# A graph network's seam between two layers: the last layer norm ahead of the selections, other places for rows and casts, and a transpose left to a store

## The chip, the cores and the metric

The kernel runs on one core of a Trainium2 chip. The metric is the device time of one execution in microseconds (us), as a median over runs. One execution is also taken with the hardware profiler; all times inside the kernel come from that one and count from the start of its span.

The core has a matrix engine (TensorE, PE in the profile, with PEld for its weight loads), VectorE (DVE), ScalarE (ACT), GpSimd (POOL), SyncE (SP), and 16 DMA engines. Every engine works through its own list of instructions in order and waits on semaphores. In this kernel POOL and SP do little but issue transfers: SP the loads, POOL the stores.

## The reference

Two layers of a graph network act on 3327 nodes with 1024 features; `adj` is a 3327 x 3327 matrix, mostly zeros, with weights on its edges. Cut to what matters:

```python
# layer 0
h = maximum(layernorm(x), 0)
support = quantised(relu(quantised(h) @ quantised(weight)))
x = x + adj @ support * scales
# layer 1: graph attention, 8 heads of 64
h = maximum(layernorm(x), 0)
Wh = einsum('nf,hfd->hnd', h, W)
e_src, e_dst = (Wh . a1), (Wh . a2)              # one number per head and node
e = leaky_relu(e_src[:, :, None] + e_dst[:, None, :], 0.2)
att = softmax(where(adj > 0, e, -9e15), axis=-1)
enc = elu(einsum('hnm,hmd->hnd', att, Wh))       # heads side by side: 512 per node
x = x + mlp(enc)                                 # 512 -> 256 -> 256 -> 512 -> 1024
```

## The kernel before

The nodes are padded to 26 tiles of 128 rows. The work runs in four stages.

**Stage 1** (to about 147 us) makes the quantised support of all nodes, kept on chip as `s_int` (26 tiles). **Stage 2** (its last product ends at about 957 us; the heads of its last two tiles follow) loops over 26 tiles `t`. For each tile the product `adj @ support` (L443) runs over the 26 column tiles in four parts of 7, 6, 7 and 6. A part is loaded as `at` (SP, L177, three buffers), split into a rounded half `hi` (ACT, L179) and a rest `lo` (DVE, L183), and tested for edges into a byte mask `mk` (DVE, L184) that is stored to `mask_d` (POOL, L188). The product's result is scaled (L451, L452) and added to `xt` (L453), which is stored to `x1_d`. The function `normalised` (L145 to L152) then makes the layer norm `y`: statistics, six short steps on one column (`lnv`, a square root on ACT, `lnr`, `lnq`, ...), and one pass over the 1024 features.

`heads(t, y)` is called one tile late, so that tile `t - 1` goes through its heads while the product of tile `t` runs. It transposes `y` on PE (L380), copies with ReLU into `ht` (ACT, L381), multiplies with the weights of the heads (`whm`, 16 matmuls at L384), copies to `wht` (L386), and forms `src` and `dst` (DVE, L391 and L392): 8 numbers per node, one per head. `dst` goes negated into `ndst`, which stays on chip. `src` is transposed on PE (`sp`, L398), copied by ACT (`srct`, L400) and stored by POOL (L403), so that `src_d` holds one row per head. `src_d` is four arrays, for the four groups of tiles in `SUBS`. The features times exp(dst) are made (`ft`, L408 and L409), split into a rounded part and a rest (`fw`, L414 and L415) and stored to `feat_d` (L423); a reordered copy `dw` (L419) goes to `dsum_d` (L427).

**Stage 3** (its first selection starts at 968 us, its last product ends about 2003) is attention. It takes 32 passes, each for one head and one group of 7 or 6 destination tiles. In each pass a row of `src_d` is loaded to all partitions as `srow` (SP, L503). For each of the 26 source tiles `j`, DVE makes a selection `sel` (L617): the mask where `srow` exceeds `ndst[j]`, else zero. PE multiplies it into 7 or 6 accumulators `acc` (L626) with the features `f_even` or `f_odd` (L493). Between these, PE works through products over all edges, `mps` (L534), from `dw` and from masks that ACT casts to `mf` (L533); `edge_steps` writes out how many of them follow each `j`. `sel` has four buffers, `srow` two. After a pass the accumulators are copied to `xs` (L638) and finished by `close`. **Stage 4** is the MLP.

What engine does what is fixed in the program; the order in which each engine gets the instructions of neighbouring tiles and stages is set by a scheduler at build time from priorities and expected durations. So the selections of stage 3 can stand in DVE's list before the end of stage 2. `keep_in_program_order` and `issue_after` bind it. Stage 3's tiles lie in memory that stage 1 and 2 used: with `reuse_waits="tile"` a new tile waits for the last use of just those old tiles that it overlaps. Pools take their place in the order in which they are opened. In the kernel before the order is `f1`, `sel`, `srow`, `mf`, `md`, `s3`.

Of the kernel before, what the change touches and what calls it, by code (L numbers as in the profile page):

```python
# [1 line left out]

# [6 lines left out]
F32 = mybir.dt.float32  # L9
# [5 lines left out]
ALU = mybir.AluOpType  # L15
# [4 lines left out]
P = 128  # L20
# [7 lines left out]
NH = 8  # L28
# [14 lines left out]
SUBS = [range(0, 7), range(7, 13), range(13, 20), range(20, 26)]  # L43
# [16 lines left out]
def two_layer_kernel(  # L60
# [23 lines left out]
    nc = tc.nc  # L84
# [5 lines left out]
    ident = const.tile([P, P], F32, name="ident")  # L90
# [54 lines left out]
    def normalised(dst, src):  # L145

        stats = small.tile([P, FC, 6], F32, tag="stats", name="stats")
        statistics(stats, src)
        mv = small.tile([P, 2], F32, tag="mv", name="mv")
        nc.vector.bn_aggr(mv, stats.rearrange("p c s -> p (c s)"))  # L150
        r = inverse_std(mv[:, 1:2], 1, EPS, "ln")
        nc.vector.tensor_scalar(dst, src, mv[:, 0:1], r, ALU.subtract, ALU.mult)  # L152

    def normaliser(mv, n, eps, factor, tag):

# [12 lines left out]
    with tc.tile_pool(name="wh", bufs=1, reuse_waits="tile") as whp, tc.tile_pool(  # L168
# [201 lines left out]
        with tc.tile_pool(name="s2", bufs=2, reuse_waits="tile") as s2, tc.tile_pool(  # L370
            name="s2_tp", bufs=2, space=PSUM, reuse_waits="tile"
        ) as tp_ps, tc.tile_pool(name="s2_wh", bufs=2, space=PSUM, reuse_waits="tile") as wh_ps:

            def heads(t, h):
                ht = s2.tile([P, KF, P], F32, name="ht", bufs=1)
                for g in range(KF // 4):
                    tp = tp_ps.tile([P, 4, P], F32, tag="tp2", name="tp2")
                    for q in range(4):
                        k = 4 * g + q
                        nc.tensor.transpose(tp[:, q, :], h[:, k * P : (k + 1) * P], ident)  # L380
                    nc.scalar.activation(ht[:, 4 * g : 4 * g + 4, :], tp, AF.Relu)  # L381
                whm = wh_ps.tile([P, EMB], F32, name="whm")
                for k in range(KF):
                    nc.tensor.matmul(whm, ht[:, k, :], whead[:, k, :], start=(k == 0), stop=(k == KF - 1))  # L384
                wht = s2.tile([P, EMB], F32, name="wht", bufs=1)
                nc.scalar.copy(wht, whm)  # L386
                src = small.tile([P, NH], F32, name="src")
                dst = small.tile([P, NH], F32, name="dst")
                for a_t, e in ((a1_t, src), (a2_t, dst)):
                    prod = s2.tile([P, EMB], F32, name="prod", bufs=1)  # L390
                    nc.vector.tensor_tensor(prod, wht, a_t, ALU.mult)  # L391
                    nc.vector.tensor_reduce(  # L392
                        e, prod.rearrange("p (h d) -> p h d", d=HD), AX.X, ALU.add
                    )
                nc.vector.tensor_scalar(ndst[:, t], dst, -1.0, None, ALU.mult)
                nc.scalar.activation(ratio[:, t], src, AF.Exp, scale=1.0 - SLOPE)
                sp = tp_ps.tile([P, 4, P], F32, tag="tp2", name="sp")
                nc.tensor.transpose(sp[:NH, 0, :], src, ident)  # L398
                srct = s2.tile([NH, P], F32, name="srct")
                nc.scalar.copy(srct, sp[:NH, 0, :])  # L400
                for sub, d in zip(SUBS, src_d):
                    if t in sub:
                        nc.gpsimd.dma_start(d[:, (t - sub[0]) * P : (t - sub[0] + 1) * P], srct)  # L403

                ft = s2.tile([P, NH, 2, HC], F32, name="ft", bufs=1)
                wh3 = wht.rearrange("p (h d) -> p h d", d=HD)
                for q, slope in enumerate((1.0, SLOPE)):
                    nc.scalar.activation(ft[:, :, q, HD], dst, AF.Exp, scale=slope)  # L408
                    nc.vector.tensor_tensor(  # L409
                        ft[:, :, q, :HD], wh3, ft[:, :, q, HD:].to_broadcast([P, NH, HD]), ALU.mult  # L410
                    )
                fw = s2.tile([P, NH, 2, 2 * HC], F32R, name="fw", bufs=1)
                f2 = ft.rearrange("p h q c -> p h (q c)")
                nc.scalar.copy(fw[:, :, 0], f2)  # L414
                nc.vector.tensor_tensor(fw[:, :, 1], f2, fw[:, :, 0].bitcast(F32), ALU.subtract)  # L415

                dw = s2.tile([P, NPAIR, 2, 2, HC], F32R, name="dw", bufs=1)
                for q in range(2):
                    nc.scalar.copy(  # L419
                        dw[:, :, q],  # L420
                        fw[:, :, q, HC:].bitcast(F32).rearrange("p (g e) c -> p g e c", e=2),
                    )
                nc.gpsimd.dma_start(  # L423
                    feat_d[t].rearrange("h p c -> p h c"),
                    fw.bitcast(F32).rearrange("p h q c -> p h (q c)"),
                )
                nc.gpsimd.dma_start(  # L427
                    dsum_d[t].rearrange("g p c -> p g c"),
                    dw.bitcast(F32).rearrange("p g q e c -> p g (q e c)"),
                )  # L430

            before = None
            for t in range(T):
                xt = s2.tile([P, F], F32, name="xt2")
                load_rows(xt, x, t)
                mm = mm_ps.tile([P, F], F32, tag="mm", name="mm2")
                for js in PARTS:
                    hi, lo = part
                    part = next(columns, None)
                    for q, j in enumerate(js):  # L440
                        for which in (hi, lo):
                            for c in range(FC):
                                nc.tensor.matmul(  # L443
                                    mm[:, c * 512 : (c + 1) * 512],
                                    which[:, q, :],
                                    s_int[j][:, c * 512 : (c + 1) * 512],
                                    start=(j == 0 and which is hi),
                                    stop=(j == T - 1 and which is lo),
                                )
                y = s2.tile([P, F], F32, name="y")  # L450
                nc.scalar.activation(y, mm, AF.Copy, scale=r_asf)  # L451
                nc.vector.tensor_scalar(y, y, asf_t, sup_delta, ALU.mult, ALU.mult)  # L452
                nc.vector.tensor_tensor(xt, xt, y, ALU.add)  # L453
                nc.gpsimd.dma_start(x1_d[t * P : (t + 1) * P, :], xt)
                normalised(y, xt)
                if before is not None:
                    heads(*before)
                before = (t, y)
            heads(*before)
# [15 lines left out]
    LATE = 2 * T + START  # L475
    with ExitStack() as wide, tc.tile_pool(name="f1", bufs=1, reuse_waits="tile") as f1p, tc.tile_pool(
        name="sel", bufs=4, reuse_waits="tile"
    ) as selp, tc.tile_pool(name="srow", bufs=2, reuse_waits="tile") as srowp, tc.tile_pool(name="mf", bufs=2, reuse_waits="tile") as mfp, tc.tile_pool(
        name="md", bufs=2, reuse_waits="tile"
    ) as mdp, tc.tile_pool(name="s3", bufs=1, reuse_waits="tile") as s3, tc.tile_pool(  # L480
        name="s3_acc", bufs=7, space=PSUM, reuse_waits="tile"
    ) as acc_ps, tc.tile_pool(name="s3_m", bufs=1, space=PSUM, reuse_waits="tile") as m_ps:
        f_odd = f1p.tile([P, T, HW], F32R, name="f_odd")
# [11 lines left out]
        def load_mask(si, sub):  # L495
            for b, t in enumerate(sub):
                nc.sync.dma_start(masks[si][:, b], mask_d[t])

        def load_src(i):
            c, g, e, si = attends[i]  # L500
            nb = len(halves[c][si])
            srow = srowp.tile([P, 7, P], F32, name="srow")
            nc.sync.dma_start(  # L503
                srow[:, :nb].rearrange("p b i -> p (b i)"),
                src_d[2 * c + si][2 * g + e].partition_broadcast(P),
            )
            return srow
# [77 lines left out]
            )  # L585

        old, young = PARTS[:3], [range(20, 24), range(24, 25), range(25, 26)]
        load_mask(0, SUBS[0])
        srow = load_src(0)
        load_features(f_even, feat_d, 0, old)  # L590
        load_features(dw, dsum_d, 0, old)
        load_mask(1, SUBS[1])
# [4 lines left out]
        for i, (c, g, e, si) in enumerate(attends):  # L597
            h = 2 * g + e
# [5 lines left out]
            for j in range(T):  # L604
# [8 lines left out]
                if n in (STEPS * NPAIR - T, STEPS * NPAIR):  # L613
                    si1 = (n - (STEPS * NPAIR - T)) // T
                    load_mask(si1, halves[1][si1])
                sel = selp.tile([P, 7, P], F32R, tag="sel", name="sel")
                nc.vector.scalar_tensor_tensor(  # L617
                    sel[:, :nb],
                    srow[:, :nb],
                    ndst[:, j, h : h + 1],  # L620
                    mask[:, :, j, :],
                    ALU.is_gt,
                    ALU.mult,
                )
                for b in range(nb):
                    nc.tensor.matmul(  # L626
                        accs[b], sel[:, b, :], f[:, j, :], start=(j == 0), stop=(j == T - 1)
# [159 lines left out]
```

## Time and profile before

| What | us |
|---|---|
| median of 3 runs | 2317.66 (2315.4 to 2319.2) |
| the profiled execution, its own time | 2316.48 |
| its span in the profile | 2314.7 |
| PE busy | 2252.5 (97%) |
| DVE busy | 1567.1 (68%) |
| ACT busy | 1003.0 (43%) |
| POOL busy (issuing left out) | 119.0 (5%) |

The 1.8 us between the profiled time and the span lie outside the profile. A group's row in the profile gives the line of the kernel, the engine, the operation, output and inputs by the program's names, its busy time and its mean; after `<-` stands what released it from waiting. The name of an operand is that of its tile, with buffer numbers left out.

### The profile page before, as it was taken

To read this page: it belongs to the slowest core of one execution; us is meant where nothing else is said; L and a number is where in the kernel's file an instruction comes from. 1 tells how busy PE (TensorE), PEld (TensorE's weight loads), DVE (VectorE), ACT (ScalarE), POOL (GpSimd) and SP (SyncE) were. 2 spreads that over 40 slices of the span, in tenths; PEclk is the share of its full clock that TensorE was granted. 3 is DMA by queue.
4 is the path that set the end of the run, shared out by engine and by line. 5 is a ranking of instruction groups with operands and counts; after the bars stand their busy time and mean duration, and the time that the engine had idled before them with its cause. 6 is when DMAs were issued, how large, how long until landed. Compare 5 with 4: busy or idle time off the path is not lost. (4 is left out here: it accounts for less than half of the span.)

```text
span 2314.7 us, 32013 instructions
## 1 busy us (share of the span) xinstructions
PE 2252.5 (97%) x12884; PEld 1788.4 (77%) x12896; DVE 1567.1 (68%) x2090; ACT 1003.0 (43%) x1654; POOL 119.0 (5%) x173
## 2 busy tenths in 40 slices
PE   4999999999999999899999999999999999999999
PEld 2467777777777777589999999999999999644444
DVE  7845555555555555487999999999999999812211
ACT  4743334333333333346555555555555555311110
POOL 0000011011110110100000000000000000000000
PEclk9999999999999999999999999999999999999999
DMA  6324444444444444743324241545242332433311
GB/s 231 128 90 149 147 159 135 154 157 149 152 152 137 165 155 144 278 145 112 112 73 147 80 146 45 197 156 162 79 143 83 117 105 71 152 109 114 131 56 55
DMA packets 150302, 304.94 MB, mean 132 GB/s; under 512 B 10173, under 2 KB 91021, under 8 KB 150153
## 3 DMA queue, kind: packets, MB, share of 16 engines
q1 hardware_dynamic: 130248, 229.72, 29.7%
q0 software_dynamic: 19904, 73.17, 9.7%
q8 instruction: 101, 1.65, 0.3%
q14 instruction: 49, 0.39, 0.1%
HBM read 216.07 MB, written 86.79 MB: 131 GB/s over the span
## 5 line engine op out<-in xcount | busy, mean ns | idle before, releaser
L617 DVE SCALAR_TENSOR_TENSOR sel<-srow,ndst,mask 128x896 fp32r<-128x896 f32 (+1 forms) x832 | 869.6, 1082 | 61.2 <-PE acc L626 49.7
L534 PE MATMUL mps<-dw,mf 128*128 128x260 f32 x2704 | 462.7, 284 | 0.0
L443 PE MATMUL mm<-s_int,hi 128*128 128x512 f32 x1352 | 433.0, 399 | 0.0
L443 PE MATMUL mm<-s_int,lo 128*128 128x512 f32 x1352 | 421.6, 391 | 0.0
L626 PE MATMUL acc<-f_even,sel 128*128 128x260 f32 x2704 | 403.9, 284 | 1.4 <-DVE sel L617 1.3
L533 ACT CAST mf<-mask 128x1664 fp32r<-128x1664 uint8 x208 | 330.0, 1588 | 167.1 <-PE mps L534 129.3
L626 PE MATMUL acc<-f_odd,sel 128*128 128x260 f32 x2704 | 393.9, 285 | 6.9 <-DVE sel L617 6.8
L534 PEld LDWEIGHTS mps<-dw,mf 128*128 128x128 f32 x2704 | 379.8, 188 | 9.3 <-ACT part L538 8.4
L626 PEld LDWEIGHTS acc<-f_odd,sel 128*128 128x128 f32 x2704 | 352.6, 188 | 15.9 <-DVE sel L617 12.2
L626 PEld LDWEIGHTS acc<-f_even,sel 128*128 128x128 f32 x2704 | 356.7, 188 | 5.9 <-DVE sel L617 2.8
L443 PEld LDWEIGHTS mm<-s_int,lo 128*128 128x128 f32 x1352 | 253.8, 188 | 57.6 <-issue 5.7
L443 PEld LDWEIGHTS mm<-s_int,hi 128*128 128x128 f32 x1352 | 252.1, 188 | 55.6 <-issue 5.7
L184 DVE TENSOR_SCALAR mk<-at 128x896 uint8<-128x896 f32 x104 | 61.7, 593 | 262.6 <-DMA at<-in_adj_t 261.9
L179 ACT CAST hi<-at 128x896 fp32r<-128x896 f32 x104 | 92.7, 891 | 328.7 <-PE mm L443 294.8
L384 PE MATMUL whm<-whead,ht 128*128 128x512 f32 x416 | 186.9, 602 | 0.8 <-ACT ht L381 0.8
L731 PE MATMUL o<-weights,h 128*128 128x512 f32 x416 | 179.7, 592 | 0.0
L731 PEld LDWEIGHTS o<-weights,h 128*128 128x128 f32 x416 | 79.0, 190 | 99.1 <-issue 99.0
L384 PEld LDWEIGHTS whm<-whead,ht 128*128 128x128 f32 x416 | 77.5, 191 | 98.1 <-issue 87.7
L183 DVE TENSOR_TENSOR lo<-at,hi 128x896 fp32r<-128x896 f32 x104 | 106.6, 1025 | 51.3 <-ACT hi L179 39.9
L538 ACT COPY part<-mps 128x260 f32<-128x260 f32 x104 | 39.1, 376 | 216.3 <-PE mps L534 216.3
L741 DVE TENSOR_TENSOR yo<-o,nodes 128x1024 f32<-128x1024 f32 (+1 forms) x27 | 31.8, 1182 | 146.0 <-PE o L731 146.0
L332 PE MATMUL mm<-w_int,xqt 128*128 128x512 bf16 x404 | 98.3, 393 | 9.5 <-DVE w_int L319 7.3
(128 smaller groups left out, 1566.9 us busy)
## 6 DMA issues: line engine op xcount, KB each, us to landing
feat_d<-fw POOLq DMA_DIRECT2D x26, 1040.0 KB, 5.3
f_even<-feat_d SPq DMA_DIRECT2D x7, 3380.0 KB, 12.8
f_odd<-feat_d SPq DMA_DIRECT2D x7, 3380.0 KB, 13.6
at<-in_adj_t SPq DMA_DIRECT2D x52, 448.0 KB, 3.9
at<-in_adj_t SPq DMA_DIRECT2D x52, 384.0 KB, 3.1
mask<-mask_d SPq DMA_DIRECT2D x39, 416.0 KB, 7.7
dw<-dsum_d SPq DMA_DIRECT2D x16, 910.0 KB, 5.1
dsum_d<-dw POOLq DMA_DIRECT2D x26, 520.0 KB, 6.5
```

The lines of the kernel that those rows point to most:

```text
L179: ins = nc.scalar.copy(hi, at)
L183: nc.vector.tensor_tensor(lo, at, hi.bitcast(F32), ALU.subtract)
L184: nc.vector.tensor_scalar(mk[:, r], at, 0.0, None, ALU.is_gt)
L332: nc.tensor.matmul(mm[:, c * 512 : (c + 1) * 512], xqts[t][:, k, :], w_int[:, k, c * 512 : (c + 1) * 512], start=(k == 0), stop=(k == KF - 1),
L384: nc.tensor.matmul(whm, ht[:, k, :], whead[:, k, :], start=(k == 0), stop=(k == KF - 1))
L443: nc.tensor.matmul(mm[:, c * 512 : (c + 1) * 512], which[:, q, :], s_int[j][:, c * 512 : (c + 1) * 512], start=(j == 0 and which is hi), s ...
L533: nc.scalar.copy(mf, mask[:, j : j + TH, :])
L534: nc.tensor.matmul(ps, mf[:, j % TH, :], dw[:, j, :], start=(j == 0), stop=(j == T - 1))
L538: nc.scalar.copy(part[:, i % 7], ps.rearrange("p (q c) -> p q c", q=2))
L617: nc.vector.scalar_tensor_tensor(sel[:, :nb], srow[:, :nb], ndst[:, j, h : h + 1], mask[:, :, j, :], ALU.is_gt, ALU.mult,)
L626: nc.tensor.matmul(accs[b], sel[:, b, :], f[:, j, :], start=(j == 0), stop=(j == T - 1))
L731: nc.tensor.matmul(ps[:, c * 512 : (c + 1) * 512], h3[:, k, q * P : (q + 1) * P], w4[:, k, c * 512 : (c + 1) * 512], start=(k == 0), stop= ...
```

## The change

1. The end of a layer norm is handed out as `ln`, and all selections of the first pass (`i == 0`) have to be issued after the last one of these.
2. `srow` no longer has one pool with two buffers but two pools with one buffer, opened after `s3`. Odd passes use `srow1` and even ones `srow0`. With that `mf`, `md` and `s3` move forward by the two buffers' room. The first row is also asked for ahead of the first masks in the program.
3. `src` is no longer transposed on PE and copied by ACT: POOL's store writes its 8 columns as rows, element by element.

As built, the first `srow` load stands on SP's list within stage 2 (in tile 8) and waits for the stores of the first seven tiles of `src`. The second stands behind the last load of tile 25's `dw` and waits for ACT. The first `mf` casts stand on ACT's list where they stood, and the first group of `mps` on PE's list follows 17 source tiles instead of 14. After the second pass the orders of the engines are the same as before, but for a few instructions at the end of attention.

```diff
-        nc.vector.tensor_scalar(dst, src, mv[:, 0:1], r, ALU.subtract, ALU.mult)
+        return nc.vector.tensor_scalar(dst, src, mv[:, 0:1], r, ALU.subtract, ALU.mult)
...
-                sp = tp_ps.tile([P, 4, P], F32, tag="tp2", name="sp")
-                nc.tensor.transpose(sp[:NH, 0, :], src, ident)
-                srct = s2.tile([NH, P], F32, name="srct")
-                nc.scalar.copy(srct, sp[:NH, 0, :])
-                for sub, d in zip(SUBS, src_d):
-                    if t in sub:
-                        nc.gpsimd.dma_start(d[:, (t - sub[0]) * P : (t - sub[0] + 1) * P], srct)
+                with nc.allow_non_contiguous_dma(reason="a thousand elements, transposed"):
+                    for sub, d in zip(SUBS, src_d):
+                        if t in sub:
+                            r = slice((t - sub[0]) * P, (t - sub[0] + 1) * P)
+                            nc.gpsimd.dma_start(d[:, r].rearrange("h p -> p h"), src)
...
-                normalised(y, xt)
+                ln = normalised(y, xt)
...
-    ) as selp, tc.tile_pool(name="srow", bufs=2, reuse_waits="tile") as srowp, tc.tile_pool(name="mf", bufs=2, reuse_waits="tile") as mfp, tc.tile_pool(
+    ) as selp, tc.tile_pool(name="mf", bufs=2, reuse_waits="tile") as mfp, tc.tile_pool(
         name="md", bufs=2, reuse_waits="tile"
     ) as mdp, tc.tile_pool(name="s3", bufs=1, reuse_waits="tile") as s3, tc.tile_pool(
+        name="srow1", bufs=1, reuse_waits="tile"
+    ) as srow1, tc.tile_pool(name="srow0", bufs=1, reuse_waits="tile") as srow0, tc.tile_pool(
...
-            srow = srowp.tile([P, 7, P], F32, name="srow")
+            srow = (srow1 if i % 2 else srow0).tile([P, 7, P], F32, tag="srow", name="srow")
...
+        srow = load_src(0)
         load_mask(0, SUBS[0])
-        srow = load_src(0)
...
-                nc.vector.scalar_tensor_tensor(
-                    sel[:, :nb],
...
+                with tc.issue_after(ln.ins) if i == 0 else nullcontext():
+                    nc.vector.scalar_tensor_tensor(
+                        sel[:, :nb],
```

More of the change, by code (lines that the diff above doesn't have):

```diff
@@ L1 @@
-from contextlib import ExitStack
+from contextlib import ExitStack, nullcontext
 import concourse.bass as bass
@@ L616, in two_layer_kernel @@
                 sel = selp.tile([P, 7, P], F32R, tag="sel", name="sel")
-                nc.vector.scalar_tensor_tensor(
-                    sel[:, :nb],
[L619 to L624, printed above, removed]
+                with tc.issue_after(ln.ins) if i == 0 else nullcontext():
+                    nc.vector.scalar_tensor_tensor(
+                        sel[:, :nb],
+                        srow[:, :nb],
+                        ndst[:, j, h : h + 1],
+                        mask[:, :, j, :],
+                        ALU.is_gt,
+                        ALU.mult,
+                    )
                 for b in range(nb):
```

## The prediction

> **What bounds the kernel now.** I read first the page's slices, 57.9 us each: the rows are tenths of busy time.
>
> ```profile
> PE   4999999999999999899999999999999999999999
> DVE  7845555555555555487999999999999999812211
> DMA  6324444444444444743324241545242332433311
> ```
>
> TensorE (PE) is full from the second slice on, except in the seventeenth (926 to 984 us), where the DMA row has its peak. That slice holds the seam between layer 0 and attention, which is where the diff is. The page's chain of waits starts only at 1983 us and says nothing about the seam. Between 190 and 957 us, windows show PE busy without a gap. So an edit pays in two ways: it takes work from PE, or it closes the hole at the seam. Next, windows over the seam; the columns are stretch, length, busy us of PE, PEld, DVE, ACT and POOL, granted clock, DMA share, GB/s.
>
> ```profile
> 957.00:967.00 10.00, 8.49 (x27) 3.95 (x25) 3.69 (x6) 4.21 (x7) 0.55 (x1) 1.00 1.08 370
> 967.00:975.00 8.00, 0.37 (x1) 0.08 (x1) 6.59 (x13) 1.62 (x3) 0.00 (x0) 0.71 1.06 375
> 975.00:989.00 14.00, 10.92 (x27) 5.48 (x27) 6.01 (x9) 4.77 (x11) 2.24 (x3) 0.80 0.90 315
> 989.00:1000.00 11.00, 9.64 (x70) 8.54 (x69) 10.92 (x14) 5.67 (x8) 2.23 (x3) 1.00 0.93 304
> ```
>
> PE does next to nothing for 8 us, and its clock falls to 0.71. The waits say why:
>
> ```profile
> PE sp L398 <- DVE lnr L136: 8.1, 1, 8.1
> ...
> DVE sel L617 <- DMA srow<-src_d: 5.9, 1, 5.9
> DVE prod L391 <- ACT wht L386: 5.5, 1, 5.5
> ...
> PE sp L398 <- DVE src L392: 2.2, 1, 2.2
> ```
>
> The transpose `sp` of tile 24 waits 8.1 us on VectorE (DVE). DVE itself stood 5.9 us for the first `srow` row, because a selection `sel` is queued ahead of the last layer norm. The timeline of DVE (start, duration) shows that order:
>
> ```profile
> 962.34 0.15 DVE L130 TENSOR_SCALAR lnv<-mv 128x1 f32<-128x1 f32 x1
> 968.40 2.21 DVE L617 SCALAR_TENSOR_TENSOR sel<-srow,ndst,mask 128x896 fp32r<-128x896 f32 x2 [5.91 <-DMA srow<-src_d]
> 970.54 0.15 DVE L132 RECIPROCAL lnr<-lns 128x1 f32<-128x1 f32 x1
> ...
> 974.91 0.81 DVE L152 TENSOR_SCALAR y<-xt,mv,lnr 128x1024 f32<-128x1024 f32 x1
> ...
> 995.57 5.40 DVE L617 SCALAR_TENSOR_TENSOR sel<-srow,ndst,mask 128x896 fp32r<-128x896 f32 x5
> ```
>
> The last `y` is done at 975.7; nothing of heads(25) can start on PE before. From 995.57 on DVE makes one `sel` after another at 1.04 us (26 in the first pass), and PE follows it until it catches up. After 1020 us `sel` waits for PE instead, so what the seam gains stays gained.
>
> The change also takes `sp` out of PE's full stretch. Timeline of PE there, then the two `whm` groups of the seam:
>
> ```profile
> 618.69 0.39 PE L443 MATMUL mm<-s_int,lo 128*128 128x512 f32 x1
> 619.01 0.27 PE L398 MATMUL sp<-ident,src 128*8 128x128 f32 x1
> 619.03 0.48 PE L443 MATMUL mm<-s_int,lo 128*128 128x512 f32 x1
> 619.35 0.63 PE L443 MATMUL mm<-s_int,hi 128*128 128x512 f32 x2
> ...
> 959.18 7.13 PE L384 MATMUL whm<-whead,ht 128*128 128x512 f32 x16 [0.82 <-ACT ht L381]
> ...
> 977.69 8.59 PE L384 MATMUL whm<-whead,ht 128*128 128x512 f32 x16
> ```
>
> A pair of L443 products comes every 0.454 us. The pair around `sp` takes 619.35 - 618.69 = 0.66: `sp` costs PE 0.20 us, not its printed 0.27, since matmuls overlap.
>
> **The Trainium skill.** "TensorE: Matmul & The Clock Gate", Part 1: after an idle window of about 3.4 us the array falls to half clock until it has been busy as long. The trace agrees: after 8.1 us of waiting the same 16 products took 8.59 instead of 7.13 us. "DMA: Bandwidth & Descriptors", Rules for kernel authors: a non-contiguous last dimension becomes one descriptor per element, and a transpose by a plain rearranged pattern is advised against (a factor of 19). The kernel before has no such store, so its trace neither confirms nor denies that. The same page, Anatomy of one DMA: about 2.0 us plus bytes / 436e3 us. For `feat_d` (1.065 MB) that gives 4.4, and the trace has 5.4 at a quiet moment (593.6 us).
>
> **Part 1: no `sp`, no `srct`.** 24 of the 26 `sp` lie in PE's full stretch: 24 x 0.20 = 4.8 us off the path. The 26 copies of 0.256 us on ScalarE (ACT) were hidden behind PE and give nothing by themselves. The `sp` of tiles 24 and 25 belong to part 2.
>
> **Part 2: last LN first.** In the changed order the six small steps and `y` follow `lnv` directly. An undisturbed tile takes 930.83 to 933.04 = 2.2 us from `lnv` to the end of `y`; so 962.34 + 2.2 = 964.6 instead of 975.7. On PE `sp` no longer separates heads(24) from heads(25): `whm` of tile 24 ends at 966.3, the 8 transposes take 1.03 (967.3), ACT copies `wht`, then `ht` (0.59 + 0.55), and `whm` of tile 25 runs from about 967.6 to 974.8 at full clock, instead of to 986.3. Then DVE in its new order, with durations of its own rows (sel 1.13, prod 0.69, reduce 0.69, ft 1.29, fw 1.24): sel, sel, prod, sel, reduce, sel, prod, reduce reach 972.0; ft waits for the exponentials (973.5), fw for ACT's cast (975.9); then prod, sel, reduce, sel, prod, sel, reduce, sel for tile 25 (983.2), ft, sel, sel, fw (988). The eleventh `sel` starts at 987.9. Before, the eighth started at 995.57, so the eleventh at 995.57 + 3 x 1.08 = 998.8. **Gain 10.9 us**, between 10 and 12 by what one takes for a `sel` (1.04 to 1.15). DVE's work is the same; what goes is 5.9 + 5.5 + some 2 us of standing, less about 2 that appears while it waits for ACT. PE now waits more for `sel` 6 to 10 (some 4 us in short pieces), which this count contains, as it follows DVE. The change moves PE's first `mps` burst from behind 14 to behind 17 tiles; the number of products is the same.
>
> **Part 3: other homes.** `srow0` lies behind the tiles of stage 2, so its row of 448 KB is asked for in tile 8 of layer 0. There SP waits for tile 6's `src`, stored at 397.2 in the trace before. With a landing of about 3.3 us that is 400, and the next `at` load queued behind it was issued at 401.3: free. Its transfer may push one `at` load by 448 KB / 370 GB/s = 1.2 us, against 4.5 us of slack (the load that follows a `src` store landed at 595.4, its `lo` was ready at 597.3 and PE began that part at 601.8). Without the early row `sel` would still have to wait for it; so part 2 needs part 3. Mask block 0 was asked for from 939.4 and landed within 12 us each, so it is there at 964.6; the first features (945.7 + 14.7) are there at 974.8. `srow1` overlaps the old `dw` and so is asked for last on SP, behind `f_odd` (free after the last `prod`, about 980), the features and the `dw` of tile 25. Stored at about 988 to 989, these land after 5 to 9 us; `srow1` is asked for at 994 to 998 and lands 3 to 5 us later. DVE wants it at 987.9 + 16 x 1.04 = 1004.5 and PE two later. Taken as free; bound 0 to 4 us lost. Casts `mf` are early (991 against a first use near 996): nothing.
>
> **Part 4: `src` stored transposed.** 26 stores on POOL's queue go from 8 runs to 1024 elements of 4 bytes. Issue on POOL: near the 0.91 us of `enc_d` (896 runs of 256 bytes) instead of 0.53; POOL is 5% busy. Landing: `enc_d` took about 3.1 us, 8 runs took 1.6, so (3.1 - 1.6) / 888 x 1024 = 1.7, together 3.3 us as an estimate. The store now starts some 0.9 us earlier (it waits for `reduce`, not for PE and ACT). So it starts near 396.3 in that tile; the next `at` load follows 5.0 us later, `feat_d` 6.4, and the window from 619.9 to 623.9 shows the DMA engines empty but for the store. Cost nothing; if that cover were gone, the bounds are 0 and 24 tiles times what exceeds 5.0 + 4.5 us. Nor can it gain beyond part 1.
>
> **Sum.** 4.8 + 10.9 = 15.7 us. Profiled execution: 2316.5 (span 2314.7) to 2300.8; the median of the runs is 1.2 above it: 2317.7 - 15.7 = **2302.0**.
>
> **Rivals.** (a) *As summed*, 2302 (2299 to 2306): chance 0.78. (b) *The transfers become the bound*: DMA share is 0.9 or more from 957 to 1000, so tile 25's features and `srow1` may come no earlier than now plus their queue. If `srow1` lands at 1010, PE gets 4.8 + 5 us: about 2308. For: SP waited up to 11.6 us for `feat_d`. Against: `f_odd`, its competitor, starts 9 us sooner too. 0.12. (c) *Element stores hold up layer 0 (slower)*: at 64 elements per DMA engine, a landing beyond 9.5 us delays `at` past its slack; the whole gain is gone when each tile loses 15.7 / 24 = 0.65, at 10.15 us, or (10.15 - 1.6) / 64 = 134 ns per element, against 1.5 / 55.5 = 27 that `enc_d` gives. At 12 us: 24 x 2.5 = 60 lost, about 2362. For: the skill's advice. Against: 4 KB only, in an empty stretch. 0.05. (d) *The order does not hold*, because `sel` still waits for something late, or gains more than counted: 2310 or 2297: 0.05.
>
> **Numbers.** The range 2296 to 2309 takes in (a), (b) and the upper end of (d). This kernel can be told from no change at about 0.2% (4.6 us): faster 0.94, within 0.02, slower 0.04.
>
> **What would show it.** No `sp`; pairs of L443 without a 0.2 us bump, so the last one ends near 952.5; no `sel` wait for `srow`; last `y` done 7 us after the last product, `whm` of tile 25 at 7.1 us, clock 1.0 over the seam; then DVE's unbroken run of `sel` (the eleventh) starts 30.6 us after the last product, before, its eleventh began after 41.5. Wrong if DVE or PE waits on a DMA in the first two passes, if `at` makes `hi` or `lo` late, or if attention after 1020 us changes length.

## The result and the profile after

The changed kernel takes 2385.71 us (median of 4 runs, 2384.99 to 2386.45) against 2317.9 (2315.4 to 2319.2) beside it: ratio 1.0294, 95% interval 1.0276 to 1.0312. It is 67.8 us slower; 15.7 us faster was predicted. The profiled execution took 2386.45 us, its span 2384.4. Numbers of lines have moved: the products of layer 0 are now L441, `sel` is L620, `acc` L629, `mps` L535, `fw` L412 and L413.

The page's slices first, now 59.6 us each:

```profile
PE   4999999899999999978999999999999999999999
DVE  7744455345544544576899999999999999812211
DMA  6334554565555455593324242464324242423321
```

The hole at the seam is still there in PE's row (a 7 and an 8, in slices 18 and 19, 1013 to 1133 us), and layer 0 ahead of it is no longer free of gaps. The DMA row is higher all through layer 0. PE's waits (in total, times, longest, us) name the new gap:

```profile
PE mm L441 <- DVE lo L183: 41.6, 21, 7.1
PE acc L629 <- DVE sel L620: 17.0, 15, 8.1
...
PE mps L535 <- DMA dw<-dsum_d: 7.4, 2, 6.9
```

The first and the last were not in the trace of before, and the 8.1 us of `sp` is gone. Behind `lo` stands a transfer. A group's row (busy, mean ns | idle ahead of it) and then the transfers with their median from issue to landing:

```profile
L184 DVE TENSOR_SCALAR mk<-at 128x896 uint8<-128x896 f32 x104 | 61.6, 593 | 412.8 <-DMA at<-in_adj_t 412.7
...
feat_d<-fw POOLq DMA_DIRECT2D x26, 1040.0 KB, 11.6
dsum_d<-dw POOLq DMA_DIRECT2D x26, 520.0 KB, 12.0
...
src_d<-src POOLq DMA_DIRECT2D x26, 4.0 KB, 10.1
```

DVE's idle time ahead of this group was 262.6 us before. The store of `src`, 4 KB, lands after 10.1 us where 3.3 was estimated; it took 1.6 from `srct`. `feat_d`, issued while it is under way, went from 5.3 to 11.6.

One tile in the timeline (start, duration):

```profile
620.08 0.90 POOL L401 DMA_DIRECT2D src_d<-src  x1 [5.62 <-DVE src L392]
...
623.84 17.29 SPq L177 DMA_DIRECT2D at<-in_adj_t  x3
...
632.07 0.61 PE L441 MATMUL mm<-s_int,hi 128*128 128x512 f32 x2
633.24 0.56 DVE L184 TENSOR_SCALAR mk<-at 128x768 uint8<-128x768 f32 x1 [8.05 <-DMA at<-in_adj_t]
633.71 0.95 DVE L183 TENSOR_TENSOR lo<-at,hi 128x768 fp32r<-128x768 f32 x1
634.72 0.73 PE L441 MATMUL mm<-s_int,lo 128*128 128x512 f32 x2 [2.03 <-DVE lo L183]
...
635.75 0.77 PE L441 MATMUL mm<-s_int,lo 128*128 128x512 f32 x2
636.33 1.05 PE L441 MATMUL mm<-s_int,hi 128*128 128x512 f32 x2
637.18 1.05 PE L441 MATMUL mm<-s_int,lo 128*128 128x512 f32 x2
```

`at` is asked for at 623.84, 3.8 us behind the store, and is there only at 633.2, 9.4 us later (the rows of `at` in before have 3.1 and 3.9). PE has no work from 632.7 on and loses 2.03 us. Then its pairs come 0.85 us apart instead of 0.454, until 639.6: from 635.75 to 640.08 six pairs take 4.33 instead of 2.72 us, 1.6 more. Windows over the same stretch (stretch, length, busy us of PE, PEld, DVE, ACT and POOL, clock, DMA share, GB/s) show both:

```profile
616.00:624.00 8.00, 8.00 (x37) 6.62 (x36) 7.17 (x18) 4.43 (x9) 0.90 (x1) 1.00 0.29 82
624.00:632.00 8.00, 8.00 (x37) 6.64 (x36) 1.18 (x1) 2.12 (x4) 1.65 (x2) 1.00 0.61 28
632.00:640.00 8.00, 5.97 (x20) 4.44 (x19) 2.28 (x4) 0.76 (x1) 0.00 (x0) 0.79 0.80 278
```

In the second one the DMA engines are busy for 61% of the time and move 28 GB/s, though 384 KB of `at` and 1.5 MB of features are asked for. In the third the clock is 0.79. The DMA queues of two stretches (packets, MB, share of the 16 engines; q0 is POOL's queue, q1 SP's) tell more:

```profile
q0 software_dynamic: 32, 0.00, 12.2%
...
q1 hardware_dynamic: 47, 0.14, 49.8%
```

The first line is from 619.9 to 623.8 us: all packets of the element store, of which the last ends at 622.3. The second is all that is on record from 622.4 to 630.2, when the store lands: packets of `at`, which take half of the engines' time for 0.14 MB. So the store's own packets are soon over, but until it has landed, other transfers hardly move.

The longest wait for `lo`, 7.1 us, came only once and needs the second edit too. SP's list has the first `srow` load there; it waits for tile 6's store, which lands at 419.9, and the next `at` stands behind it (waits of SP, timeline of PE):

```profile
SPq L504 <- DMA src_d<-src: 11.1, 1, 11.1
...
430.90 1.22 PE L441 MATMUL mm<-s_int,lo 128*128 128x512 f32 x2 [7.09 <-DVE lo L183]
```

So layer 0 grows. Its last product ends at 1018.0 instead of 957.3, 60.7 us later. The rest, about 8 us, is lost at the seam (windows with the same columns, moved by those 61 us from the ones shown of before):

```profile
1018.00:1028.00 10.00, 9.03 (x33) 4.67 (x31) 7.81 (x15) 4.57 (x8) 0.55 (x1) 1.00 1.06 373
1028.00:1036.00 8.00, 7.85 (x24) 4.02 (x25) 6.73 (x10) 4.13 (x9) 0.89 (x1) 1.00 1.15 347
1036.00:1050.00 14.00, 9.94 (x65) 8.81 (x63) 10.35 (x14) 1.50 (x5) 2.53 (x3) 0.88 1.06 206
1050.00:1061.00 11.00, 4.36 (x20) 4.37 (x21) 6.72 (x7) 1.06 (x1) 0.89 (x1) 0.61 1.05 188
```

The second window is what the change was made for: PE has 7.85 busy us there instead of 0.37, at full clock. But from 1036 on the GB/s fall to 206 and 188, with the DMA engines full, and the hole is back in the fourth. The timeline says what is late:

```profile
1028.15 7.13 PE L384 MATMUL whm<-whead,ht 128*128 128x512 f32 x16 [0.31 <-ACT ht L381]
...
1053.19 1.06 ACT L412 CAST fw<-ft 128x1040 fp32r<-128x1040 f32 x1 [10.95 <-DMA feat_d<-fw]
1054.28 1.24 DVE L413 TENSOR_TENSOR fw<-ft,fw 128x1040 fp32r<-128x1040 f32 x1 [7.93 <-ACT fw L412]
...
1056.64 5.57 PE L629 MATMUL acc<-f_even,sel 128*128 128x260 f32 x24 [8.15 <-DVE sel L620]
...
1062.23 1.16 ACT L417 CAST dw<-fw 128x520 fp32r<-128x520 f32 x2 [7.99 <-DMA dsum_d<-dw]
...
1082.92 0.58 PE L535 MATMUL mps<-dw,mf 128*128 128x260 f32 x1 [6.92 <-DMA dw<-dsum_d]
```

`fw` has one buffer. ACT stands 10.95 us ahead of tile 25's cast, until tile 24's `feat_d` has left the buffer; DVE waits 7.93 for the cast with all later selections queued behind, and PE 8.15 for a selection. `dw` has one buffer as well, and the same happens to it a little later: ACT waits 7.99 us for tile 24's `dsum_d`. The last load of `dw` is asked for at 1076.5 (58.6 us after layer 0's last product; 44.1 in `e3_runs32` below), and PE waits 6.92 us for it, near the end of the first pass.

### The profile page after: what moved, and what is told of

Read it like the earlier page. It is cut to its first block, busy times and chain, and to the rows that moved or that the text cites. A ratio compares the mean times of both kernels' runs of the same rounds, so it can differ in the third digit from the quotient of the medians.

```text
span 2384.4 us, 31895 instructions
## 1 busy us (share of the span) xinstructions
PE 2275.2 (95%) x12870; PEld 1806.3 (76%) x12870; DVE 1557.5 (65%) x2090; ACT 993.8 (42%) x1628; POOL 127.1 (5%) x173
## 5 line engine op out<-in xcount | busy, mean ns | idle before, releaser
L620 DVE SCALAR_TENSOR_TENSOR sel<-srow,ndst,mask 128x896 fp32r<-128x896 f32 (+1 forms) x832 | 870.0, 1081 | 66.4 <-PE acc L629 51.2
L535 PE MATMUL mps<-dw,mf 128*128 128x260 f32 x2704 | 463.5, 285 | 7.4 <-DMA dw<-dsum_d 7.4
L441 PE MATMUL mm<-s_int,lo 128*128 128x512 f32 x1352 | 430.0, 400 | 41.6 <-DVE lo L183 41.6
L441 PE MATMUL mm<-s_int,hi 128*128 128x512 f32 x1352 | 442.4, 406 | 0.0
L629 PE MATMUL acc<-f_even,sel 128*128 128x260 f32 x2704 | 407.5, 287 | 10.7 <-DVE sel L620 10.7
L629 PE MATMUL acc<-f_odd,sel 128*128 128x260 f32 x2704 | 394.4, 286 | 6.5 <-DVE sel L620 6.3
L535 PEld LDWEIGHTS mps<-dw,mf 128*128 128x128 f32 x2704 | 380.8, 189 | 16.9 <-ACT part L539 8.2
L629 PEld LDWEIGHTS acc<-f_even,sel 128*128 128x128 f32 x2704 | 360.9, 191 | 15.1 <-DVE sel L620 11.8
L629 PEld LDWEIGHTS acc<-f_odd,sel 128*128 128x128 f32 x2704 | 353.6, 189 | 14.8 <-DVE sel L620 11.1
L441 PEld LDWEIGHTS mm<-s_int,lo 128*128 128x128 f32 x1352 | 258.9, 193 | 110.1 <-DVE lo L183 50.9
L441 PEld LDWEIGHTS mm<-s_int,hi 128*128 128x128 f32 x1352 | 258.7, 193 | 59.2 <-issue 5.7
## 6 DMA issues: line engine op xcount, KB each, us to landing
feat_d<-fw POOLq DMA_DIRECT2D x26, 1040.0 KB, 11.6
```

The source lines that it names most:

```text
L441: nc.tensor.matmul(mm[:, c * 512 : (c + 1) * 512], which[:, q, :], s_int[j][:, c * 512 : (c + 1) * 512], start=(j == 0 and which is hi), s ...
L535: nc.tensor.matmul(ps, mf[:, j % TH, :], dw[:, j, :], start=(j == 0), stop=(j == T - 1))
L620: nc.vector.scalar_tensor_tensor(sel[:, :nb], srow[:, :nb], ndst[:, j, h : h + 1], mask[:, :, j, :], ALU.is_gt, ALU.mult,)
L629: nc.tensor.matmul(accs[b], sel[:, b, :], f[:, j, :], start=(j == 0), stop=(j == T - 1))
```

## The experiments

Theory: the store of single elements costs the time, in layer 0 through `at` and at the seam through `feat_d`, and the other two edits give what the prediction summed. Rivals: the other edits lose something at the seam too; or it is not the elements but POOL's queue that is slow. Each experiment is told against the kernel named with its edit.

**The two other edits without the store** (`e1_pe_transpose`: the changed kernel with this part as before).

```diff
-                            nc.gpsimd.dma_start(d[:, r].rearrange("h p -> p h"), src)
...
+                nc.tensor.transpose(sp[:NH, 0, :], src, ident)
...
+                nc.scalar.copy(srct, sp[:NH, 0, :])
...
+                        nc.gpsimd.dma_start(d[:, (t - sub[0]) * P : (t - sub[0] + 1) * P], srct)
```

> Edits 1 and 2 of the change alone: src goes back to its transpose on TensorE, the copy and the store in 8 runs. Theory (the element store holds the DMA engines for some 9 us per tile, and the at loads behind it come late): layer 0 is as long as before (last product near 957), at lands 3 to 4 us after its issue, the median is 2307 to 2315 (the seam gains some 6 us, less than the 10.9 of my sum because sp stands again between the heads of tiles 24 and 25). Rival (the moved srow load or the other places of mf hold up layer 0): layer 0 stays at about 1018 and the median at 2375 to 2385.

2312.11 us against 2318.37, ratio 0.9973 (0.9962 to 0.9985). Without the store the two gain 6.3 us, though layer 0's last product ends 1.6 us later in this profile than before (958.9 against 957.3). The loss of 60.7 us there doesn't come from them alone.

**The store alone, in the kernel before** (`e2_store_alone`: the third edit and nothing else).

> Edit 3 alone, put into the kernel before: no sp, no srct, src stored element by element; selections, rows and casts as before. Theory: the loss is all here, 2375 to 2395, with src landing at 10 us and lo awaited by TensorE about 2 us in most tiles. Rival (homes or LN order cost layer 0): 2310 to 2320.

2400.78 us, ratio 1.0358 (1.0343 to 1.0374), 6 us above the expectation; the store lands after 10.6 us. PE's waits:

```profile
PE mm L441 <- DVE lo L183: 55.6, 23, 3.8
PE tp L380 <- DVE y L152: 16.4, 1, 16.4
```

The store alone costs 82.4 us. Without the early row no wait for `lo` is longer than 3.8 us. At the seam it now stands in front of the first `srow` too, for which DVE still waits ahead of the last `y`: hence the 16.4.

**The same bytes in runs of 32** (`e3_runs32`: each partition's 8 numbers side by side in memory; the transposition is left out).

```diff
-                            nc.gpsimd.dma_start(d[:, r].rearrange("h p -> p h"), src)
+                            nc.gpsimd.dma_start(d.rearrange("h n -> (h n)")[r.start * NH : r.stop * NH].rearrange("(p h) -> p h", h=NH), src)
```

> The whole change, but the store writes 128 runs of 32 bytes, one per partition, in place of 1024 elements; what is left out is the transposition, so the attention reads its src rows from the wrong places. Theory (it is the number of elements that costs): landing near 2 to 3 us, layer 0 at 952 to 953, the median at 2299 to 2306, which is what my sum gave when the store was priced at nothing. Rival (any store from src in that place, or taking sp out of TensorE's order, costs): above 2330.

2304.64 us, ratio 0.9944 (0.9929 to 0.9959); the store lands after 1.7 us. This is the prediction without its wrong step: timeline of PE and DVE at the seam.

```profile
953.46 1.03 PE L380 MATMUL tp<-ident,y 128*128 128x128 f32 x8
...
959.87 0.81 DVE L152 TENSOR_SCALAR y<-xt,mv,lnr 128x1024 f32<-128x1024 f32 x1
...
963.63 7.13 PE L384 MATMUL whm<-whead,ht 128*128 128x512 f32 x16 [0.31 <-ACT ht L381]
...
984.90 11.78 DVE L620 SCALAR_TENSOR_TENSOR sel<-srow,ndst,mask 128x896 fp32r<-128x896 f32 x11
```

The last product ends near 953.5, `y` is done 7.2 us later, `whm` of tile 25 has full clock. The row at 984.90 begins with the eleventh selection: 31.4 us after the last product (30.6 was predicted, 41.4 was before). As the rows are read from other places, the first `srow` load stands at 209 us here, so this run says nothing on its price near 400.

**Half of the elements** (`e4_half`: four heads of eight; the other four rows are ones).

```diff
-                            nc.gpsimd.dma_start(d[:, r].rearrange("h p -> p h"), src)
+                            nc.gpsimd.dma_start(d[: NH // 2, r].rearrange("h p -> p h"), src[:, : NH // 2])
+                            nc.gpsimd.dma_start(d[NH // 2 :, r], ones[: NH // 2])
```

> The whole change, but only 4 of the 8 columns of src go out as elements (512 a tile); the rows of the other four heads get ones in 4 runs, so their values are left out. Theory (cost per element of about 8.5 us / 1024 for the DMA as a whole): landing near 1.6 + 4.3 = 5.9 us, which is done about when the next at load is issued, 5.0 us after the store; so layer 0 loses at most 0.5 us a tile and the median is 2300 to 2315. Rival (a fixed cost of such a store, not per element): landing still near 10 us, median above 2370; a loss in proportion to the elements would give about 2350.

2393.64 us, ratio 1.0329 (1.0313 to 1.0344), and the 512 elements land after 10.1 us, as 1024 do. The expectation, a price for each element, fell.

**Another queue** (`e5_act_queue`: `nc.scalar.dma_start` for the same store).

> The whole change with one word replaced: the element store is issued on ScalarE's queue instead of POOL's. Theory of shared pieces: the writes are the same, so landing is again about 10 us, at loads are as late, and the median is 2370 to 2400. Rival (POOL's making of 1024 descriptors, or feat and dsum standing behind the store in the same queue, is what costs): landing below 5 us, at on time, 2300 to 2315.

2397.22 us, ratio 1.034 (1.0325 to 1.0354); landing 11.3, and PE waits 55.6 us for `lo` again. The rival with POOL's queue fell.

**The elements further apart** (`f1_space64`, `f5_space8`) **or only one head** (`f3_one_head`). `pad_d` is a new buffer that nobody reads.

```diff
+    pad_d = dram.tile([NH, P, 16], F32, name="pad_d")   # f5: [NH, P, 2], f3: [NH, P, 1]
...
-                            nc.gpsimd.dma_start(d[:, r].rearrange("h p -> p h"), src)
+                            nc.gpsimd.dma_start(pad_d[:8, :, 0].rearrange("h p -> p h"), src[:, :8])   # f3: 1 for both 8
+                            nc.gpsimd.dma_start(d[:, r], ones[:NH])
```

> The whole change, but the 1024 elements of a tile's src go to an array of their own in which neighbours lie 64 bytes apart instead of 4; the rows that the attention reads hold ones, so its selections are left out of account. The half store had 512 elements and took 10 us all the same, so a price per element has fallen. Theory now (partial writes into the same piece of memory follow one another: with 4-byte neighbours 16 or more elements share a piece, and it is the length of that queue, not the number of elements, that costs): with no two elements in one piece landing falls to 2 to 4 us and the median to 2298 to 2308. Rival (a store of 4-byte runs has a fixed cost of some 8 us wherever it writes; or reading single words out of the partitions costs it): landing stays at 9 to 11 us and the median above 2370.

> As in the run with spacing, but only one of the 8 columns goes out, as 128 elements side by side (512 bytes in all); the rest is left out and the rows read are ones. Theory of shared pieces: each piece gets as many writes as before, so landing stays near 8 to 10 us and the median above 2360, with an eighth of the elements. Per element: landing near 2.7 us, median about 2303. Fixed cost of 4-byte runs: as with shared pieces.

> The changed kernel with the 1024 elements of the store written 8 bytes apart instead of 4, to a buffer of twice the size beside the one that is read back (the rows that attention reads are ones, so src is left out of its result). Theory (writes that fall into the same small piece of memory follow one another): half as many neighbours in a piece, so the store lands after some 1.6 + 8.5/2 = 5.9 us, below the 8.3 us at which the adjacency tile becomes late: 2303 to 2312. Rival (any spacing under 64 bytes costs the same): it lands after about 10 us again and the kernel takes over 2370.

| Kernel | elements, apart | landing, us | time, us | ratio (95%) |
|---|---|---|---|---|
| `f1_space64` | 1024, 64 bytes | 3.1 | 2303.62 | 0.9939 (0.9925 to 0.9953) |
| `f5_space8` | 1024, 8 bytes | 4.0 | 2305.6 | 0.995 (0.9936 to 0.9964) |
| `f3_one_head` | 128, 4 bytes | 8.2 | 2333.01 | 1.0068 (1.0055 to 1.0082) |

A thousand elements that do not touch land in about the 3.3 us of the estimate; an eighth of them side by side takes 8.2. For `f3_one_head` the landing came out as expected and the time, expected over 2360, did not: at 8.2 us `at` is only just late (PE waits 7.7 us for `lo`, 11 times). `f5_space8` came in under its 5.9 us. In these runs and the four below, the first `srow` load stands at 150 to 152 us and holds up no `at`.

The traces also hold every packet of the DMA engines. They divide the landing in two (medians over the tiles):

| Kernel | elements, apart | issue to the end of the store's last packet, us | from there to landing, us |
|---|---|---|---|
| after | 1024, 4 bytes | 2.2 | 7.8 |
| `f1_space64` | 1024, 64 bytes | 2.2 | 0.9 |
| `f5_space8` | 1024, 8 bytes | 2.2 | 1.7 |
| `e4_half` | 512, 4 bytes | 1.8 | 8.3 |
| `f3_one_head` | 128, 4 bytes | 1.6 | 6.6 |
| `e3_runs32` | 128 runs of 32 bytes | 1.3 | 0.4 |

The number of elements shows in the packets, and there it costs at most a microsecond. The price of touching falls behind the last packet, where the traces show only that the store hasn't landed.

The cost isn't in proportion to the neighbours in a piece of memory, so another theory was worth a test: that a store is divided among the DMA engines by partitions, and engines that share a piece of 64 bytes hold one another up (B).

**Who the neighbours are** (`f4_space4`, `g2_whole`, `g3_mixed8`, `g4_mixed4`; one execution each, read for the landing).

```diff
# f4_space4: pad_d [NH, P, 1], as f1
# g2_whole: pad_d [NH // 2, 2 * P]
+ nc.gpsimd.dma_start(pad_d.rearrange("k (p c) -> p c k", c=2), src.rearrange("p (c k) -> p c k", c=2))
# g3_mixed8: pad_d [8, 16, 2]; g4_mixed4: pad_d [8, 16, 1]
+ nc.gpsimd.dma_start(pad_d[:, :, 0:1].rearrange("b a e -> a b e"), src[:, :1])
```

> Control: all 1024 elements side by side as in the changed kernel, but written to the buffer of the spacing runs, with the rows that attention reads filled with ones. Both theories: about 10.1 us to landing, as in the changed kernel. Should it land after 3 to 5 us, the place of the buffer was the cause and not the spacing.

> As f4_space4, but the 1024 elements of 4 bytes lie so that each row of 256 takes two columns of all partitions in turn: every piece of 64 bytes is filled by 8 partitions instead of 16. Rows that attention reads are ones. Theory A (neighbouring 4-byte writes follow one another, 16 to a piece of 64 bytes): about 10 us to landing. Theory B (a store is divided among 16 engines by 8 partitions each, and two engines that share a piece of 64 bytes hold one another up): no piece is shared, so about 4 us.

> 128 elements of one head, 8 bytes apart, but neighbours come from partitions 8 apart (rows that attention reads are ones). Theory A: half the neighbours of f3_one_head (8.2 us), so 4 us or less as f5_space8. Theory B: each piece of 64 bytes is now written by 8 engines, so 8 us or more.

> 128 elements of one head side by side, neighbours from partitions 8 apart (rows that attention reads are ones). Theory A: as f3_one_head, 8.2 us. Theory B: 16 engines to a piece instead of two, so over 8.2 us.

They landed after 10.6, 8.4, 3.2 and 7.5 us. B fell in all three tests: the second lies nearer to A's 10 us than to B's 4, and neighbours from other partitions, 8 bytes apart, cost nothing. What is left is that elements of 4 bytes that touch are slow (7.5 to 10.6 us in five layouts), and with a gap of 4 bytes they aren't (3.2 and 4.0). Why a gap of one element does it stays open.

`g4_mixed4` tells something more. It took 2315.35 us in its one execution, and these are its waits:

```profile
ACT fw L414 <- DMA feat_d<-fw: 8.1, 1, 8.1
...
PE acc L631 <- DVE sel L622: 15.2, 16, 6.3
```

PE never waits for `lo`, and the last product ends at 951.8: at 7.5 us layer 0 loses nothing, but the seam does, through `fw` and then through `dw`, for which PE waits 5.4 us.

**Which edit gives the gain** (`e6_ln_alone`: the first edit in the kernel before; `e7_homes_alone`: the second, with `sp` kept; `e9_grouped_unbound` and `e8_grouped`: without and with the first edit, the second in both, and `sp` moved). In the last two DVE writes `src` of a whole group side by side; PE transposes once for each group, 4 times instead of 26, the last time behind the eleventh source tile's products of attention:

```diff
-                            nc.gpsimd.dma_start(d[:, r].rearrange("h p -> p h"), src)
+                src = srcs[0][:, t - g[0]]
...
+        nc.tensor.transpose(sp[: n * NH], srcs[:, :n].rearrange("p t h -> p (t h)"), ident)
+        nc.scalar.copy(srct[: n * NH], sp[: n * NH])
+        for b in range(n):
+            nc.gpsimd.dma_start(d[:, b * P : (b + 1) * P], srct[b * NH : (b + 1) * NH])
...
-                with tc.issue_after(ln.ins) if i == 0 else nullcontext():   # e7 and e9 only
+                with nullcontext():
```

> The first edit alone, in the kernel before: the last LN ahead of the selections, src still transposed by TensorE at the seam. Theory: the selections still wait for the row that comes out of the two transpositions, so y is earlier but the first attention product hardly is: about 2315, 2 to 3 us below the kernel before. Rival (the early LN is by itself worth what the prediction's Part 2 gave to all of the seam): 2307 to 2312.

> The second edit alone, with src still transposed by TensorE and without the LN's place being bound: about 2311 to 2313, as e1_pe_transpose with both (2312.1), since the early row frees the selections and the LN is only partly delayed by them. Rival (the two edits need one another): no gain over the kernel before, 2316 to 2319.

> A version meant to beat both: edits 1 and 2 as they are, and src transposed on TensorE but by groups: src of 6 or 7 tiles is gathered (up to 56 columns), transposed by one matmul, copied once and stored in runs of 512 bytes; the last group's transpose is put behind the first products of attention. Theory: 22 of 26 transposes leave TensorE (22 x 0.20 = 4.4 us) and none stands at the seam, so the median is 2301 to 2306, close to that of the 32-byte store (2304.6) but with the whole computation. Rival (six or seven stores in a row on POOL's queue, or the late transpose, hold something up): 2308 to 2315.

> e8_grouped without the first edit: src transposed by groups off the seam, the LN's place not bound. Theory: four selections of 1.1 us run between the steps of the last LN, so y comes some 5 us later, and the first attention product with it: 2307 to 2310 against 2304.6 with the edit. Rival (the products of attention wait for the eleventh selection whatever stands ahead of it): 2304 to 2306, no difference.

The third column reads from each profile the stretch from the end of layer 0's last product to the end of the thirtieth selection, four into the second pass, and so prices the seam alone.

| Kernel | median, us (ratio, 95%) | seam, us |
|---|---|---|
| before | 2317.1 to 2318.4 | 62.2 |
| first edit (`e6_ln_alone`) | 2314.99 (0.999, 0.9984 to 0.9997) | 60.4 |
| second edit (`e7_homes_alone`) | 2312.27 (0.998, 0.9971 to 0.9988) | 57.0 |
| both (`e1_pe_transpose`) | 2312.11 (0.9973, 0.9962 to 0.9985) | 55.5 |
| second, `sp` grouped (`e9_grouped_unbound`) | 2307.56 (0.9957, 0.9945 to 0.997) | 55.2 |
| both, `sp` grouped (`e8_grouped`) | 2304.64 (0.9946, 0.9933 to 0.996) | 52.4 |
| both, runs of 32 bytes (`e3_runs32`) | 2304.64 (0.9944, 0.9929 to 0.9959) | 53.8 |
| both, element store (after) | 2385.71 (1.0294, 1.0276 to 1.0312) | 70.0 |

In `e6_ln_alone` the first selection starts at 968.8, as before it (968.4). Not the two transpositions hold it, as was expected: tile 6, the row's last, was stored before 400 us, but in both kernels the load is asked for at 957.3 and lands at 968.0. `sp` waits nearly as long (8.1 us before):

```profile
PE sp L398 <- DVE src L392: 9.9, 2, 7.7
```

The second edit is worth more than the early LN (5.2 against 1.8 us of the seam), and `sp` has to leave the seam for the rest. That in the second edit it is the early row, and not the other places, is argued from the wait for the row and not tested. The LN's place is worth about 3 us where `sp` is gone (seam 55.2 against 52.4) and can't be told from nothing where it stays (2312.27 and 2312.11). In `e9_grouped_unbound` the four selections ahead of `y` delay it to 965.5, 12.5 us behind the last product instead of 7.2, and PE waits 3.7 us for it.

`e8_grouped` beats both kernels: it computes all that the kernel before does, 13 us faster. PE's timeline there:

```profile
952.41 1.03 PE L393 MATMUL tp<-ident,y 128*128 128x128 f32 x8
954.26 7.13 PE L397 MATMUL whm<-whead,ht 128*128 128x512 f32 x16 [0.82 <-ACT ht L394]
961.24 1.04 PE L393 MATMUL tp<-ident,y 128*128 128x128 f32 x8
962.58 7.13 PE L397 MATMUL whm<-whead,ht 128*128 128x512 f32 x16 [0.31 <-ACT ht L394]
969.15 4.76 PE L642 MATMUL acc<-f_even,sel 128*128 128x260 f32 x35
```

From the last product to the first of attention PE has no gap over 1 us.

## Why the prediction was wrong

**The step that failed is the landing in part 4**: 3.3 us, from `enc_d`'s 27 ns for a run of 256 bytes, against a measured 10.1. The trace of before had no store of touching elements of 4 bytes, and the price was carried over from runs to elements as if only their number counted. `f1_space64` shows that the number is priced about rightly (3.1 us for 1024 of them, apart); that they touch made the other 7, behind the last packet. The Trainium skill's rule, which the prediction quoted and then outvoted ("DMA: Bandwidth & Descriptors", Rules for kernel authors, against a transpose by a plain rearranged pattern), would have been the better guide: 10.1 us against 1.6 for the store of rows. Its factor of 19 is set against the DMA hardware's own transpose, which no run here uses. What the same table says of a non-contiguous last dimension, one descriptor per element, isn't what costs here: 512 and 1024 elements land alike, and 1024 apart do so in 3.1.

**Rival (c) came true, and its price was too low.** It put the limit at a landing of 9.5 us and 0.6 us for each tile at 10.1, so 14 us. Two of its terms were off, and one of part 3. The room: in most tiles `at` follows the store after 3.8 us, not 5.0 (4.6 in `e3_runs32`), so the limit is 3.8 + 4.5 = 8.3 us. As an estimate, 24 x (10.1 - 8.3) = 43 us, and PE waited 41.6; for `e2_store_alone` 24 x (10.6 - 8.3) = 55, and PE waited 55.6. The true limit seems to lie a little lower: 7.5 us cost layer 0 nothing (`g4_mixed4`), and 8.2 made its end 12.97 us later than in `e3_runs32` (`f3_one_head`, 966.43 against 953.46).

The early row, which part 3 called free on the strength of a landing of 3.3 us: the one wait of PE behind it is 7.1 of the 41.6 us, so the agreement for the changed kernel is in part luck. And the clock: the last product is 64.5 us later than in `e3_runs32` (1017.98 - 953.46). The waits are 41.6 of these. The other 22.9 fit products at half clock, as in the tile shown (1.6 us): the clock records of the trace have eleven such stretches in this loop, 44.3 us together, of which half, 22, is lost.

**What was missed at the seam.** The prediction let DVE make `fw` of tile 25 once ACT had cast it, and never asked what frees `fw`'s only buffer: `feat_d` of tile 24, hidden at 5.4 us. When the stores crawl, it frees the buffer 9.0 us after the cast's input `ft` is there (1053.2 against 1044.2), and then `dw`'s only buffer is late in the same way. That is a second limit, lower than the first: `g4_mixed4` meets it at 7.5 us, and its seam is 64.3 us instead of the 54.3 of `g3_mixed8`, which differs only by the gaps. In the changed kernel the seam got 7.8 us longer (70.0 - 62.2). Together with layer 0's 60.7 that makes 68.5 of the 70 us between the two profiled executions.

**What was right.** *Part 1* (4.8 us): the last product ends 3.9 us earlier in `e3_runs32` and 4.9 in `e8_grouped`. *Part 2* (10.9 us): the eleventh selection came 10.0 us closer to the last product (41.4 - 31.4), and the seam is 8.4 to 9.8 us shorter at the thirtieth; PE's pieces of waiting for `sel` grew from 8.0 to 12.0 us, as it said. But the part is named after the last LN, and that alone gives 2 to 3; the second edit and the missing `sp` give the rest. "Part 2 needs part 3" was right (`e6_ln_alone`). *Part 3*: in `e8_grouped` the first row is asked for at 400.3, as forecast, and lands in 4.0 us; PE waits for no transfer there or at the seam. Whether the row pushes layer 0 by the 1.2 us that the part allowed for stays open: `e1_pe_transpose` and `e7_homes_alone` end it 1.6 and 1.4 us later than before, but the ends in the seven profiles with few or no `sp` and no wait for `lo` differ by 1.7 us among themselves. So parts 1 to 3 give 2304.64 us (two kernels) where the sum had 2302.0, inside its range of 2296 to 2309.

## What to carry to other kernels

Don't carry a price per run over to single elements: ask whether a store writes touching elements of 4 bytes (measured here for 0.5 to 4 KB), and if it does, transpose on chip and store rows, gathered for several tiles to keep it cheap. A small transfer is judged by its landing and by what else is under way meanwhile, not by its bytes: look for the first load or buffer behind it, and take the tightest of these limits, which here was a single buffer at the seam and not the load in the loop. A load that is moved ahead takes its wait along: whatever stands behind it in the queue then waits too. When an order of instructions is changed together with what they wait for, test the two apart before one of them gets the credit.

## What the runs showed of the hardware that was not expected

- A store of 128 elements of 4 bytes that touch took 7.5 to 8.2 us, of 512 or 1024 such elements 10.1 to 10.6 on POOL's queue (8.4 where two columns alternate, `g2_whole`) and 11.3 on ACT's; with 4 bytes between them 3.2 (128) and 4.0 (1024), with 60 bytes 3.1. As 128 runs of 32 bytes, which also touch, the same 4 KB took 1.7.
- The time is not in the store's packets: for 1024 elements the last one ended 2.2 us after the issue, touching or not, and the landing came 7.8 us later when they touched and 0.9 when 60 bytes lay between them.
- Until such a store had landed, the DMA engines counted as busy for 61% of the time and moved 28 GB/s, with 1.9 MB waiting.
- The clock fell after a wait of only 2.03 us: some 1.5 us after its end it was halved for 3.4 us (0.52 from 636.2 to 639.6). In layer 0 of the changed kernel 11 of the 13 waits of 2 us or more had such a stretch at or near their end, and none of the 8 waits of up to 1.1 us had one; in `e2_store_alone` one of 3.14 us had none either. The Trainium skill ("TensorE: Matmul & The Clock Gate", Part 1) speaks of an idle window of about 3.4 us before the clock falls; here the measurement decides. In that loop the stretches at half clock made the waits half as dear again (22.9 beside 41.6 us).
